# Layer 3 of a four-layer convolution kernel: two lanes of depthwise taps run as whole units, and all other matrix products are gathered between the units

## The chip, the cores and the metric

The kernel runs on one core of a Trainium2 chip. The metric is the device time of one execution in microseconds (us); the times shown are medians of several executions. All data are fp32. TensorE carries out an fp32 matmul in two passes, so in the profile's counts every matmul of the program stands as two MATMUL records, each with a LDWEIGHTS record of its own.

## The reference

The network is four layers on x of shape (4, 48, 256, 256), each with a normalisation before it and a residual after it. Layers 1 and 2 are scans in four directions; layers 0 and 3 are gated feed-forward blocks with a frequency mask. Only layer 3 is touched here:

```python
h = einsum('bchw,oc->bohw', x, w_in)          # 48 -> 288 channels
h = irfft2(rfft2(h in 8x8 patches) * fft_mask) # a mask for each channel
h = depthwise 3x3 convolution of h             # nine taps a channel
x1, x2 = split(h, 2)                           # 144 channels each
y = einsum('bchw,oc->bohw', gelu(x1) * x2, w_out)
```

Since w_in acts on channels and the transform on pixels of a patch, the kernel transforms the 48 input channels first, applies w_in and the mask to the coefficients, and transforms 288 channels back.

## The kernel before: how layer 3 is tiled and what sets the order of its work

`layer3` works through steps of eight image rows, for two images (a and b) at once: 2 pairs of images x (32 full steps + 1 tail step) = 66 steps, 64 of them full. In each full step:

- `normed` (ACT, eight instructions) scales the rows into u; `turned` (TensorE, tiles pt) transposes it into xt; `waves` (tiles pf) transforms it into xf, copied out of PSUM by ACT.
- `spectrum(xf, q)`, once for each of 16 column blocks q, multiplies xf (the weights, 48x128, one for each image) by w_in (288 columns moved) into a tile pz. VectorE then multiplies by the mask into z, in two instructions (128x512 and 128x64).
- `pixels(step, g, k)` transforms z back (tiles pp) into five padded images: z_a0, z_a1 (the first 128 channels of x1 and of x2 of image a), z_b0, z_b1 (of image b), and z_m (what is left over of both). It first copies the two rows above from the step before; then ACT copies each pp tile out, in two instructions of 128x512.
- The depthwise taps. TensorE does those of z_a0, z_a1, z_m and of the lower half of z_b with diagonal 32x32 weights: a `lane` owns two of the four row groups of the array, and one round of a lane is one tap on eight 32x32 tiles. Two lanes fill the sixteen tiles. Nine rounds make a unit, which leaves its sums in a tile pd. The upper half of z_b is done by VectorE: a scaling on ACT, then eight SCALAR_TENSOR_TENSOR a half ("unit", L1220), a gelu and a product.
- `curve` (ACT gelu from pd), `gate` and `lower_gate` (VectorE products from pd, L1203 and L1187) make the gated tiles; `mixed` multiplies them by w_out (tiles po) and adds the residual on VectorE (L1269) before the store.

All of pt, pf, pz, pp, pd and po share one PSUM pool of **four buffers** (`ps_w`), handed out in the order in which they are asked for. Each engine runs its instructions in the order of the program (`manual_schedule`).

That order comes from `in_turns`: after every round of the lanes it adds 0.55 us of credit a lane, and as soon as the credit is not negative it issues the next piece of `work()` (a transpose, a transform, two q of spectra, one `pixels`, a store), each with a hand-written cost. Lane 1 starts four rounds behind lane 0. Pieces therefore fall between tap rounds in many places. `aside` deals out VectorE's taps by the same reckoning. `pixels` of an image has to wait until its last reader is through (`free`, by counts in `taken`).

Of the kernel before, what the change touches and what calls it, by code (L numbers as in the profile page):

```python
# [9 lines left out]
F32 = mybir.dt.float32  # L10
# [7 lines left out]
C = 48  # L18
# [13 lines left out]
class Net:  # L32
# [505 lines left out]
    def in_turns(self, lanes, pieces, pace, side=iter(())):  # L538

        piece, credit, count, ahead, cost = next(pieces), 0.0, 0, 0.0, 1.0
        while lanes or piece:
            moved, spent = 0, 0.0
            for k, l in enumerate(list(lanes)):
                if k == 1 and count < 4:
                    continue
                got = next(l, None)
                if got is None:
                    lanes.remove(l)  # L550
                moved += bool(got)
            count += moved > 0
            spent += 0.54 * moved
            credit = min(credit + pace * moved, 2.0)
            while piece and piece[0]() and (credit >= 0 or not moved):
                piece[2]()
                credit = max(credit - piece[1], -5.0)
                moved, spent = 1, spent + piece[1] - sum(piece[3:])
                piece = next(pieces, None)
            ahead, idle = max(min(ahead + spent, 2.5), -4.0), 0  # L560
            while ahead > 0 or not moved:
                cost = next(side, None)
                if cost:
                    ahead, moved = ahead - cost, 1
                elif cost is None or moved or idle > 20:
                    break
                else:
                    idle += 1
            assert moved or not lanes

    def aside(self, units):

        later, begun = [], set()

        def tick():
            if later:
                later[0][0] -= 1
            while later and later[0][0] <= 0:  # L580
                _, cost, work = later.pop(0)
                work()
                if cost:
                    yield cost

        def begin(k):
            if k < len(units) and k not in begun and units[k][0]():
                begun.add(k)
                units[k][1]()

        for k, (_, _, taps, last) in enumerate(units):
            wait = 0 if k in begun else 2
            while wait:
                begin(k)
                wait -= k in begun
                yield from tick()
                yield 0.0
            for i, (cost, tap) in enumerate(taps):
                if i >= len(taps) - 5:
                    begin(k + 1)  # L600
                tap()
                yield cost
                yield from tick()
            later += [list(e) for e in last]
        while later:
            yield from tick()
            yield 0.0

# [343 lines left out]
    def layer3(self, x, scs):  # L952
# [9 lines left out]
        tail = lambda step: step[1] == H // RB  # L962
        with ExitStack() as st:
# [9 lines left out]
            mk_in = wp.tile([40, 2 * HD], F32, name="mk_in")  # L973
# [4 lines left out]
            mask = wp.tile([128, 1, 2 * HD], F32, name="mask")  # L978
            pm = ps_w.tile([128, 2, MM], F32, name="pm", tag="w")
            nc.tensor.matmul(pm[:, 0, : 2 * HD], self.sel, mk_in, start=True, stop=True)  # L980
            nc.vector.tensor_copy(mask[:, 0], pm[:, 0, : 2 * HD])
# [81 lines left out]
            def turned(u):  # L1063
                xt = mid.tile([128, NQ, 112], F32, name="xt")
                for q0 in range(0, NQ, 8):
                    pt = ps_w.tile([128, 2, MM], F32, name="pt", tag="w")
                    for q in range(8):
                        nc.tensor.transpose(  # L1068
                            pt[:, q // 4, q % 4 * 112 : (q % 4 + 1) * 112],
                            u[:, q0 + q].rearrange("p k e h w -> p (k e h w)"), self.ident[0:112, 0:112],  # L1070
                        )
                    nc.scalar.copy(
                        xt[:, q0 : q0 + 8, :].rearrange("p (k q) c -> p k (q c)", k=2), pt[:, :, 0 : 4 * 112]
                    )
                return xt

            def waves(xt):
                xf = mid.tile([112, NQ, 128], F32, name="xf", tag="u")
                for q0 in range(0, NQ, 8):
                    pf = ps_w.tile([128, 2, 8, 64], F32, name="pf", tag="w")  # L1080
                    for q in range(8):
# [7 lines left out]
                    nc.scalar.copy(  # L1089
                        xf[:, q0 : q0 + 8, :].rearrange("p q (l f) -> p q l f", l=2),  # L1090
# [4 lines left out]
            z = wp.tile([128, NQ, 4 * HD], F32, name="z")  # L1095

            def spectrum(xf, q):

                pz = ps_w.tile([128, 2, MM], F32, name="pz", tag="w")
                for b in range(2):  # L1100
                    s = slice(64 * b, 64 * b + C)
                    nc.tensor.matmul(pz[:, b, 0 : 2 * HD], xf[s, q, :], wi[s, :], start=True, stop=True)  # L1102
                n = 2 * NM
                nc.vector.tensor_tensor(  # L1104
                    z[:, q, 0 : 2 * n].rearrange("p (b c) -> p b c", b=2), pz[:, :, 0:n],
                    mask[:, :, 0:n].to_broadcast([128, 2, n]), ALU.mult,
                )
                nc.vector.tensor_tensor(  # L1108
                    z[:, q, 2 * n :].rearrange("p (h b c) -> p b h c", h=2, b=2),
                    pz[:, :, n : 2 * HD].rearrange("p b (h c) -> p b h c", h=2),  # L1110
                    mask[:, :, n:].rearrange("p o (h c) -> p o h c", h=2).to_broadcast([128, 2, 2, NR]),
                    ALU.mult,
                )
# [3 lines left out]
            def pixels(step, g, k):  # L1117

                n, at, old = (64, 64 * (step[1] % 2), 64 - 64 * (step[1] % 2)) if g == "m" else (128, 0, 0)
# [5 lines left out]
                if tail(step):  # L1125
                    nc.gpsimd.memset(t[:, 2, 1 : W + 1], 0.0)
                    return


                for q0 in range(0, NQ, 8):  # L1130
                    pp = ps_w.tile([128, 2, 8, 64], F32, name="pp", tag="w")
                    for q in range(8):
                        for c in range(n // 64):
                            to, q1 = (slice(64 * (q % 2), 64 * (q % 2) + 64), q // 2) if n == 64 else (
                                slice(64 * c, 64 * c + 64), q
                            )
                            for l in range(2):
                                f = slice(64 * l, 64 * l + 64)
                                nc.tensor.matmul(  # L1139
                                    pp[to, l, q1, :], z[f, q0 + q, k * NM + 64 * c : k * NM + 64 * c + 64],  # L1140
# [3 lines left out]
                        "p h (q j l w) -> p j l q h w", j=128 // n, l=2, w=8  # L1144
                    )
                    for j in range(128 // n):
                        for l in range(2):
                            nc.scalar.copy(  # L1148
                                to[:, j, l], pp[n * j : n * j + n, l, 0 : n // 16].rearrange("p q (h w) -> p q h w", w=8)
                            )  # L1150
# [350 lines left out]
```

## Time and profile before

| | us |
|---|---|
| median of 3 runs (13403.15 to 13455.93) | 13437.11 |
| span of the profiled execution | 13427.3 |
| layers 0 to 2, until about | 8632 |
| layer 3 before its first tap | 59 |
| layer 3, first tap to the end | 4736 |

The profiled execution lies within the spread of the runs. The profile is read by engine (PE is a TensorE matmul, PEld a weight load, DVE VectorE, ACT ScalarE, POOL GpSimd), with busy times as unions of spans. A busy PE is not PE at its peak: a matmul counts from its start to its modelled end, so one short record after another can fill the time. A timeline row has start, length, engine, line, operation, tiles, shape and count, with the idle time before it and what ended that in brackets.

### The profile page before, as it was taken

How to read it: one execution, taken by the hardware profiler on the slowest of the kernel's cores; microseconds unless marked ns; L12 is line 12 of the kernel's file. 1: busy time of each engine (PE TensorE's matmuls, PEld its weight loads, DVE VectorE, ACT ScalarE, POOL GpSimd, SP SyncE). 2: the span in 40 equal slices, each digit the busy share in tenths (PEclk: the TensorE clock that was granted, in tenths of full speed). 3: DMA queues.
4: the chain of work that ended last, by engine and by line, in shares of the span. 5: the costliest groups of instructions: out<-in, count | busy, mean ns of one | idle time of the engine just before them, and what ended most of it. 6: DMA issues, size and time to landing. Idle time of an engine off the chain costs nothing.

```text
span 13427.3 us, 418750 instructions
## 1 busy us (share of the span) xinstructions
PE 12419.8 (92%) x195144; PEld 7348.8 (55%) x195144; DVE 7184.5 (54%) x11691; ACT 3956.8 (29%) x4845; POOL 1336.4 (10%) x977
## 2 busy tenths in 40 slices
PE   2999899998999899999998999799999999999999
PEld 1333333335777677767776777544444454444444
DVE  6777777773333334543333346555555555555555
ACT  1444444442223100012231000044444344444443
POOL 0110010100000003520000025300000000000000
PEclk9999999998999999999999999899999999999999
DMA  7222222225755877977658769501011010011010
GB/s 171 56 56 56 57 54 56 57 49 110 154 138 151 169 151 161 229 165 152 138 154 166 154 147 227 133 19 27 22 27 27 22 28 20 22 27 27 22 27 20
DMA packets 1170327, 1224.12 MB, mean 91 GB/s; under 512 B 1027669, under 2 KB 1031757, under 8 KB 1107725
## 3 DMA queue, kind: packets, MB, share of 16 engines
q1 hardware_dynamic: 1070476, 649.55, 24.8%
q0 software_dynamic: 87488, 445.55, 11.5%
q10 hardware_dynamic: 10624, 102.24, 4.4%
q8 instruction: 1532, 25.10, 0.8%
q14 instruction: 207, 1.69, 0.1%
HBM read 699.76 MB, written 497.42 MB: 89 GB/s over the span
## 4 chain that ended last, share of the span: by engine, by line
PE 47%; ACT 4%; DVE 3%; issue 2%; DMA 0%; SPq 0%; POOL 0%; ACTq 0%; DVEq 0%; POOLq 0%
PE acc L732 20%; PE pd L1160 11%; PE pz L1102 4%; PE pp L1139 4%; PE pd L1176 4%; PE po L1256 2%; ACT u L1056 2%; PE pf L1085 1%; DVE g_b L1187 1%; PE pt L1068 1%; PE po L1246 1%; DVE z L1104 1%; ACT z_a L1148 1%; ACT gl L1186 1%; DVE acc L1220 1%
## 5 line engine op out<-in xcount | busy, mean ns | idle before, releaser
L732 PE MATMUL acc<-line,w_down 96*96 96x256 f32 x12240 | 2692.9, 382 | 52.8 <-ACT line L802 31.5
L732 PEld LDWEIGHTS acc<-line,w_down 96*96 96x96 f32 x12240 | 2008.2, 164 | 729.9 <-DVE line L811 34.2
L1160 PE MATMUL pd<-z_a,diag 32*32 32x512 f32 x37152 | 1862.3, 606 | 45.1 <-issue 31.1
L308 PE MATMUL pd<-main,diag 32*32 32x512 f32 x36864 | 1432.8, 623 | 80.0 <-issue 76.4
L1220 DVE SCALAR_TENSOR_TENSOR acc<-z_b,wd,acc 128x1024 f32<-128x1024 f32 (+1 forms) x1056 | 1328.7, 1260 | 307.0 <-ACT acc L1217 275.0
L732 PE MATMUL acc<-line,w_right 96*96 96x256 f32 x6120 | 1339.4, 379 | 82.0 <-DVE line L882 60.0
L732 PE MATMUL acc<-line,w_left 96*96 96x256 f32 x6120 | 1362.5, 384 | 31.2 <-DVE line L923 31.2
L345 DVE SCALAR_TENSOR_TENSOR acc<-rest,wd,acc 128x1024 f32<-128x1024 f32 x1024 | 1256.7, 1284 | 125.7 <-ACT acc L339 125.4
L732 PEld LDWEIGHTS acc<-line,w_right 96*96 96x96 f32 x6120 | 999.0, 163 | 412.0 <-DVE line L882 61.3
L732 PEld LDWEIGHTS acc<-line,w_left 96*96 96x96 f32 x6120 | 1007.8, 165 | 377.5 <-DVE line L923 47.1
L1176 PE MATMUL pd<-z_b,diag 32*32 32x512 f32 x18432 | 1068.5, 604 | 33.8 <-DVE z L1108 22.0
L1104 DVE TENSOR_TENSOR z<-pz,mask 128x512 f32<-128x512 f32 x1024 | 701.6, 685 | 482.0 <-PE pz L1102 477.4
L811 DVE TENSOR_TENSOR line<-acc,in 96x256 f32<-96x256 f32 x1020 | 429.2, 421 | 961.7 <-PE acc L732 951.6
L308 PEld LDWEIGHTS pd<-main,diag 32*32 32x32 f32 x36864 | 504.7, 105 | 795.6 <-issue 681.0
L885 DVE SCALAR_TENSOR_TENSOR line<-acc,b_right,in 96x256 f32<-96x256 f32 x1020 | 489.4, 480 | 834.9 <-PE acc L732 834.1
L1160 PEld LDWEIGHTS pd<-z_a,diag 32*32 32x32 f32 x37152 | 594.0, 103 | 596.4 <-issue 437.9
L846 DVE SCALAR_TENSOR_TENSOR line<-acc,b_down,in 96x256 f32<-96x256 f32 x992 | 476.0, 480 | 810.8 <-PE acc L732 810.8
L120 ACT ACTIVATE nrm<-nrm 96x2 f32<-96x2 f32 (+2 forms) x5 | 1.0, 203 | 2987.7 <-DVE nrm L119 2987.7
L1139 PEld LDWEIGHTS pp<-c_inv,z 64*64 64x64 f32 x36864 | 603.5, 136 | 465.9 <-issue 262.9
L1139 PE MATMUL pp<-c_inv,z 64*64 64x64 f32 x36864 | 676.1, 222 | 171.7 <-DVE g_b L1187 82.6
L923 DVE SCALAR_TENSOR_TENSOR line<-acc,b_left,in 96x256 f32<-96x256 f32 x992 | 475.8, 480 | 563.8 <-PE acc L732 563.8
L933 POOL TENSOR_TENSOR blk<-blk,line 96x1024 f32<-96x1024 f32 x248 | 705.3, 2872 | 644.0 <-DVE line L923 644.0
(158 smaller groups left out, 12383.8 us busy)
## 6 DMA issues: line engine op xcount, KB each, us to landing
blk<-x ACTq DMA_DIRECT2D x64, 1536.0 KB, 20.2
in<-x SPq DMA_DIRECT2D x248, 384.0 KB, 11.1
dn<-line POOLq DMA_DIRECT2D x124, 768.0 KB, 9.3
rt<-line POOLq DMA_DIRECT2D x124, 768.0 KB, 9.5
in<-rt SPq DMA_DIRECT2D x124, 768.0 KB, 12.6
in<-dn SPq DMA_DIRECT2D x120, 768.0 KB, 5.8
in<-up SPq DMA_DIRECT2D x240, 384.0 KB, 9.9
up<-blk POOLq DMA_DIRECT2D x56, 1536.0 KB, 14.3
```

What stands on the lines that cost most here:

```text
L308: nc.tensor.matmul(pd[32 * j : 32 * j + 32, i], diag[s, t, :], z[s, R2 * j + t // 3 : R2 * j + t // 3 + R2, t % 3 : t % 3 + W], start=(t = ...
L345: nc.vector.scalar_tensor_tensor(to, at(t, r), wd[:, 1, t : t + 1], to, ALU.mult, ALU.add)
L732: self.nc.tensor.matmul(acc, w[:, t, :], carry[:, :, t : t + m], start=(t == 0), stop=(t == 2))
L846: nc.vector.scalar_tensor_tensor(inner(line), acc, bd, new[r], ALU.add, ALU.add)
L885: nc.vector.scalar_tensor_tensor(blocks(inner(line)), blocks(acc), br, new, ALU.add, ALU.add)
L933: (nc.vector if w0 == 0 else nc.gpsimd).tensor_tensor(part, part, inner(ln[:, f::2])[..., lo:hi].rearrange("p w i h -> p i h w"), ALU.add)
L1102: nc.tensor.matmul(pz[:, b, 0 : 2 * HD], xf[s, q, :], wi[s, :], start=True, stop=True)
L1104: nc.vector.tensor_tensor(z[:, q, 0 : 2 * n].rearrange("p (b c) -> p b c", b=2), pz[:, :, 0:n], mask[:, :, 0:n].to_broadcast([128, 2, n]), ...
L1139: nc.tensor.matmul(pp[to, l, q1, :], z[f, q0 + q, k * NM + 64 * c : k * NM + 64 * c + 64], self.inv1[f, :], start=True, stop=True,)
L1160: nc.tensor.matmul(pd[32 * j : 32 * j + 32, i, 0:n, :], diag[s, 2 if g == "m" else half, t, :], zt[g][s, R2 * j + t // 3 : R2 * j + t // 3 ...
L1176: nc.tensor.matmul(pd[to, i], diag[s, half, t, :], zt[f"b{half}"][s, R2 * j + t // 3 : R2 * j + t // 3 + R2, t % 3 : t % 3 + W], start=(t ...
L1220: nc.vector.scalar_tensor_tensor(made[0], at(t), wd[:, half, t : t + 1], made[0], ALU.mult, ALU.add)
```

## The change

- `in_turns` and `aside` are gone from layer 3. The order is written out. `together(k)` runs the nine rounds of one unit of each lane side by side, with five of VectorE's taps dealt out among them; everything else is issued in one group between two such calls. Two steps (an even and an odd one) have seven units a lane, so seven groups.
- z becomes three tiles: zs[0] and zs[1] (the 128 channels of each half, for 16 q and both images) and zr (the rest). `spectrum(xf, k, q0)` makes half k for four q, with w_in's 128 columns moved for each weight; `spectrum_rest` makes the rest for all 16 q, with 32 columns moved. VectorE's mask products have 1024 elements a partition each, nine a step.
- `pixels` takes a string of engines: "A" has ACT copy a pp tile out, "D" VectorE; the same holds for `turned` and `waves`.
- xf no longer shares its buffer with u; a repeated mask (mask_r) is made once at the start.

```diff
-            side = self.aside([unit(s, k) for s in steps for k in range(2)])
-            self.in_turns([lane(0), lane(1)], work(), 0.55, side)
+            def together(k, aside=None):
+                going = [unit(l, *units[l][k]) for l in range(2)]
+                for t in range(9):
+                    for g in list(going):
+                        if next(g, None) is None:
+                            going.remove(g)
+                    if t == 1 and aside is not None:
+                        aside()
+                    if due and (t + 1) * 5 // 9 > t * 5 // 9:
+                        due.pop(0)[1]()
...
+            for n, step in enumerate(steps):
+                even = n % 2 == 0
+                pixels(step, "a0", "AD")
+                if not even:
+                    spectra(n, 1)
+                upper(n, 0, "AD")
+                if even:
+                    turn(n + 1, "AD")
+                together(k, None if even else lambda: ready(n + 1))
+                pixels(step, "a1", "DD")
+                store(n - 1)
+                if fresh(n + 2):
+                    fetch(steps[n + 2])
+                pixels_rest(step)
+                if even:
+                    wave(n + 1, "AA")
+                else:
+                    turn(n + 1, "AA")
+                together(k + 1)
+                upper(n, 1, "AA")
+                if even:
+                    spectra(n + 1, 0)
+                    spectra_rest(n + 1)
+                else:
+                    wave(n + 1, "AA")
+                    spectra(n + 1, 0, slice(0, 2))
+                together(k + 2)
+                k += 3
+                if not even:
+                    spectra(n + 1, 0, slice(2, None))
+                    spectra_rest(n + 1)
+                    spectra(n + 1, 1)
+                    together(k, lambda: ready(n + 2))
+                    k += 1
...
+            zs = [wp.tile([128, NQ, 2, NM], F32, name=f"z{k}", tag=f"z{k}") for k in range(2)]
+            zr = wp.tile([128, NQ, 4 * NR], F32, name="zr")
+            def spectrum(xf, k, q0):
+                pz = ps_w.tile([128, 2, 4, NM], F32, name="pz", tag="w")
+                for q in range(4):
+                    for b in range(2):
+                        s = slice(64 * b, 64 * b + C)
+                        nc.tensor.matmul(
+                            pz[:, b, q, :], xf[s, q0 + q, :], wi[s, NM * k : NM * k + NM], start=True, stop=True
+                        )
+                nc.vector.tensor_tensor(
+                    zs[k][:, q0 : q0 + 4].rearrange("p q b c -> p b q c"), pz,
+                    mask[:, :, :, NM * k : NM * k + NM].to_broadcast([128, 2, 4, NM]), ALU.mult,
+                )
+            def spectrum_rest(xf):
+                pz = ps_w.tile([128, 2, 2 * NQ, NR], F32, name="pz", tag="w")
+                for q in range(NQ):
+                    for b in range(2):
+                        s = slice(64 * b, 64 * b + C)
+                        nc.tensor.matmul(
+                            pz[:, b, 2 * q : 2 * q + 2, :], xf[s, q, :], wi[s, 2 * NM :], start=True, stop=True
+                        )
```

`upper` is `pixels` of z_b0 or z_b1 and the scaling of its upper half; `unit` is nine rounds of one lane with the gelu or gate that follows. An even step gives lane 0 four units (a0, a1, b, m) and lane 1 three, an odd step the reverse, so in the odd steps' units the lanes work on different images.

## The prediction

> **What bounds it now.** The windows view of the stretch from layer 3's first tap (8691) to 13420 comes first: us, then busy time of PE, PEld, DVE, ACT, POOL, then granted clock.
>
> ```profile
> 8691.00:13420.00 4729.00, 4428.70 (x119101) 2256.73 (x119093) 2704.24 (x3974) 1947.55 (x3136) 5.71 (x15) 0.99 0.10 24
> ```
>
> TensorE is busy 94%, VectorE 57%, ACT 41%, and DMA 10%: TensorE sets the pace. 4729 us over 64 full steps are **73.9 us a step**. But busy hides how much of it is work, so I price each kind of run from its start to the start of the next kind, in a stretch of the timeline with no wait:
>
> ```profile
> 10067.10 1.24 PE L1102 MATMUL pz<-wi,xf 48*128 48x288 f32 x8
> 10068.27 1.14 PE L1176 MATMUL pd<-z_b,diag 32*32 32x512 f32 x32
> 10069.34 1.24 PE L1102 MATMUL pz<-wi,xf 48*128 48x288 f32 x8
> ...
> 10072.75 1.14 PE L1176 MATMUL pd<-z_b,diag 32*32 32x512 f32 x32
> 10073.83 2.11 PE L1139 MATMUL pp<-c_inv,z 64*64 64x64 f32 x128
> 10075.87 1.14 PE L1176 MATMUL pd<-z_b,diag 32*32 32x512 f32 x32
> ```
>
> Two q of spectra take 1.17 us (10068.27 - 10067.10), one tap round of both lanes 1.07, a `pixels` 2.04. The chain of waits, in order of time, has the rest (start, us, what):
>
> ```profile
> 10023.85 1.86 PE po L1246 x4
> 10025.71 4.46 PE po L1256 x62
> ...
> 10037.01 1.15 PE pd L1160 x32
> 10038.17 0.82 issue
> 10038.99 1.15 PE pd L1160 x32
> 10040.14 1.68 PE pt L1068 x16
> ```
>
> A store takes 6.3, a transpose 1.7; pf has as many 64x64 records as a `pixels` (8192 / 64 = 128), so 2.0. In a step there are 37152 + 9288 + 18432 = 64872 tap records / 64 / 32 = 31.7 rounds. Unhindered, a step is 31.7 x 1.07 = 33.9 (taps) + 8 x 1.17 = 9.4 (pz) + 4.5 x 2.04 = 9.2 (pp) + 2.0 + 1.7 + 6.3 = **62.5 us. The other 11.4 are waits.** One of them:
>
> ```profile
> 10013.55 1.16 PE L1139 MATMUL pp<-c_inv,z 64*64 64x64 f32 x64
> 10014.38 1.01 ACT L1186 ACTIVATE gl<-pd 64x1024 f32<-64x1024 f32 x1
> 10015.42 0.62 ACT L1124 COPY z_b<-z_b 128x512 f32<-128x512 f32 x1
> 10015.43 1.22 DVE L1187 TENSOR_TENSOR g_b<-gl,pd 64x1024 f32<-64x1024 f32 x1 [8.40 <-ACT gl L1186]
> 10016.07 1.18 ACT L1148 COPY z_b<-pp 128x512 f32<-128x512 f32 x2
> 10016.71 1.02 PEld L1139 LDWEIGHTS pp<-c_inv,z 64*64 64x64 f32 x64 [2.13 <-DVE g_b L1187]
> 10016.71 1.16 PE L1139 MATMUL pp<-c_inv,z 64*64 64x64 f32 x64 [1.99 <-DVE g_b L1187]
> ```
>
> The second pp tile needs the PSUM buffer of a pd; the gate that frees it waits for a gelu, which stood behind eight `normed` instructions on ACT. PE stands still for 2 us in the middle of a `pixels`. The shape recurs: few PSUM buffers, freed by an engine that has something else in its queue.
>
> **Part 1, taps.** Seven units of nine rounds in two steps. Rounds side by side are no cheaper than rounds with pieces between them (1.07 against 4.40 / 4 = 1.10 for four in a row at 10030.17), so no gain is counted: 9 x 1.075 + 0.1 = 9.8 us a unit, **34.3 a step** against 33.9.
>
> **Part 2, spectra.** Before: 64 weight loads a step, 288 columns moved for each. After: 3 x 64 = 192, with 128, 128 and 32. Here the Trainium skill speaks against the change (TensorE: Matmul & The Clock Gate, "LDWEIGHTS (loading the stationary operand)": the load's time goes by the columns of the weights, P / 1.2 ns, whatever the rows). By it each of the 128 added loads is 107 ns; one behind another and exposed, that is +13.7 us a step, and the change would lose. The row next to it is pp: 64 columns loaded and 64 moved, as the new ones have 128 and 128. Its 128 records on four tiles are 32 in succession and take 2.04 us, 0.064 each with the drain. The four 512-column passes at 10023.85 give 1.86 / 4 / 512 = 0.9 ns a column, so 64 moved columns alone are 0.058: the load lies behind the matmul. PEld of pz tells that two loads run at once, one for each image's row group (mean 189 ns each, 351.8 us busy for 4096, so 86 ns each). I take twice pp's pace, 0.115 us a pair: a call for four q has 8 pairs, 0.92 us; the rest has 32 pairs, bound by the load, 3.7 us. A step: 8 x 0.92 + 3.7 + two drains of 0.2 = **11.4** against 9.4. Bounds: 10.5 (0.107 a pair) to 21 (load and matmul in turn).
>
> **Part 3, PE sum.** Groups of two steps, with pp tile pairs at 2.04 (two pairs together 3.9): even 5.6 (a0, b0, pt), 11.4 (a1, store, rest, pf), 9.6 (b1, 4 calls, rest); odd 7.9 (a0, 4 calls, b0), 11.1 (a1, store, rest, pt), 6.1 (b1, pf, 2 calls), 9.4 (6 calls, rest). Sum 61.1, with 7 x 9.8 = 68.6 it is 129.7: **64.9 a step**, 2.4 above the old sum. All gain must come from the 11.4 of waits.
>
> **Part 4, waits that are left.** I walk each group with the four buffers in rotation, gelu 1.05, gate 1.2, two ACT copies of 128x512 1.2 (L1148), a DVE copy taken as L1104's 128x512 product, 0.6 to 0.7, a mask product of 1024 elements taken as L1203's, 1.2, xo 2.7 for eight.
> - Odd group 1: both pd of the b units are held by gelu + gate, one after another (2.7 and 3.9 us after the taps' end); the first pz waits 0.5, the second 0.3; b0's two tiles and both pd then each wait for a mask product (the fourth ends at 10.0). Taps at 10.1 instead of 7.9: **2.2**.
> - Odd group 3: ACT has a gelu, the rows above, four copies of b1 and the scaling of the upper half (1.22) ahead of xf's copy, which ends at 6.8. pz needs it; PE is idle from 4.2. Taps at 9.0 instead of 6.1: **2.9**.
> - Odd group 2: the second pd waits for ACT's four copies of the rest, 12.2 against 11.1: 1.1. Even group 2 likewise 0.7, even 1 0.8 (a gate frees b0's tile), even 3 0.1, odd 4 0.3.
> Sum 8.1 in two steps, **4.0 a step**. VectorE's taps never set the end: five of 1.3 us are 6.5 of a unit's 9.8, and with seven units 35 places stand for 32 taps. VectorE gains 16 x (0.69 + 0.21) - 9 x 1.2 = 3.6 us a step from the wider products and takes eight copies of 0.65; ACT loses those. Both have room (57% and 41%). What these hide costs nothing while a group's queue is shorter than its PE sum; in odd 1 and odd 3 it isn't, and that is counted.
>
> **Part 5, clock.** The windows view after the wait above:
>
> ```profile
> 10013.50:10017.70 4.20, 2.21 (x136) 2.02 (x128) 1.22 (x1) 3.66 (x6) 0.00 (x0) 1.00 0.00 0
> 10017.80:10021.20 3.40, 3.40 (x70) 1.22 (x65) 0.78 (x1) 2.42 (x3) 0.00 (x0) 0.50 0.02 5
> ```
>
> An idle gap of 2 us was followed by 3.4 us at clock 0.50. The same page of the skill ("Why this matters for your kernels") warns of gaps over about 3 us. By the rule the 2.6 us gap of odd group 3 costs nothing; by the row it can cost half of 3.4 us, 1.7 a time, 0.85 a step at the most. The measurement decides that it may happen; I take a little over half, 0.5 a step.
>
> **Sum.** 64.9 + 4.0 + 0.5 = 69.4 against 73.9: 4.5 x 64 = 288 us, so 13427 - 288 = **13,140 us** against the span, which is 10 us under the median of the runs shown. The 59 us before the first tap stay: nine mask products of 1.2 for sixteen pairs of 0.9, against two more pixel tiles and a transpose ahead of the first tap. The DMAs keep their number; `fetch` moves behind the store's four output DMAs on SP, with a landing of 5.1 us and over 40 us until ACT wants it. POOL and SP queue nothing else here.
>
> **Rivals.**
> - A, forecast: 0.70, own range 13,050 to 13,230 (1.4 us a step each way: a pair at 0.107 to 0.125 us, waits of 3 to 5).
> - B, the groups close up: waits almost vanish because the gates leave sooner than I walk. 64.9 a step is 13,427 - 576 = 12,850; halfway 12,980. For it: ACT and DVE have slack. Against it: four buffers. 0.12.
> - C, the waits move and are not removed: gelu, gate and copies of both lanes now fall due at one time, at the end of a unit. 9 us of waits a step (2.6 a group) is no change, 13,430. For it: the g_b wait above has just this shape. 0.10, half of it on a gain of over 0.5% still.
> - D, slower: **the loads are exposed.** Place: the 96 pairs of pz in a step. At 0.23 us a pair instead of 0.115 they cost 11 us more a step, of which odd 1's waits hide about 1: +10 x 64 = 640, 13,780. It decides from 0.162 a pair on (4.5 us over 96 pairs). Against it: pp. 0.05. A clock that halves after nearly every group (3.5 x 1.7 = 6 us a step, 13,490) is 0.03 more.
> - That the order isn't as described is excluded: in the changed kernel's instruction order on TensorE eighteen lots of eight tap matmuls stand in one piece.
>
> A measurement of this kernel tells 0.5% (67 us) from no change. Faster by more: 0.70 + 0.12 + 0.05 = 0.87. Within: 0.05. Slower: 0.08. The range reaches into B's half way and C's: 12,970 to 13,340.
>
> **What would show it.** Taps in runs of 288 records with about 9.8 us to the next kind; pz runs of four calls at 3.7 to 4.0 us and VectorE mask products of 1.2; a wait for an ACT copy of xf ahead of pz in odd steps; PE's sum of waits at 4 a step. Wrong would be: a pz pair over 0.16 us, a unit over 10.5, clock under 0.97 in the layer, or a DVE gate that stands behind its own taps.

## The result, and the profile after

| | us |
|---|---|
| before, median of 4 runs (13403.15 to 13455.93) | 13430.65 |
| after, median of 4 runs (13259.28 to 13288.38) | 13278.57 |
| ratio after / before, 95% interval | 0.9895 (0.9874 to 0.9917) |
| forecast | 13140 (12970 to 13340) |
| span of the profiled execution after | 13257.5, 170 less than before |

The kernel became about 1.1% faster. That lies inside the forecast's range and on its side, but the gain is about half of the 290 us that were forecast: that the range held is luck as far as the mechanism goes, for most of what took the other half was not in the forecast. First the page of after (span, busy time of the engines, clock by slices), then its windows view of layer 3 (us, busy time of PE, PEld, DVE, ACT, POOL, granted clock, DMA share, GB/s):

```profile
span 13257.5 us, 432328 instructions
PE 12356.8 (93%) x203336; PEld 8155.9 (62%) x203336; DVE 7417.3 (56%) x10766; ACT 3602.9 (27%) x4043; POOL 1336.7 (10%) x977
PEclk9999999998999999999999999889999999999999
```

```profile
8691.00:13250.00 4559.00, 4372.60 (x126990) 3054.55 (x126965) 2932.76 (x3064) 1588.13 (x2324) 5.69 (x15) 0.97 0.12 25
```

A full step now takes 4559 / 64 = 71.2 us, where it took 73.9 and 69.4 was forecast. TensorE has some 7,900 matmul records more. One figure moved that the forecast gave little room: the granted clock is 0.97 where it was 0.99.

The waits that the change aimed at did go: by the trace's records of layer 3, TensorE stood idle (stretches of over 0.15 us) for 172 us until a semaphore came before, and for 18 us after. In the groups view of the same stretch (busy us, mean ns of one, then the idle time before and what ended it), `pp` of before lost 82.6 us to the lower gate. After:

```profile
L1139 PE MATMUL pp<-c_inv,z 64*64 64x64 f32 x36761 | 674.5, 222 | 171.7 <-DVE g_b L1187 82.6 <-issue 69.7 <-DVE g_m L1203 15.8
```

```profile
L1043 DVE TENSOR_TENSOR z<-pz,mask 128x1024 f32<-128x1024 f32 x504 | 591.4, 1219 | 272.4 <-PE pz L1040 270.0
L1087 PE MATMUL pp<-c_inv,z 64*64 64x64 f32 x32512 | 557.2, 220 | 50.7 <-issue 49.3
```

The first fence is before, the second after. What is left ahead of `pp` is "issue": the engine waited for nothing that the profile shows. Of such idle time there is more than before, 164 us in the layer instead of 122. The second line above also has the wider mask product at the 1.2 us that the forecast took.

To see where the rest went, every group (all that lies between two tap runs) and every unit (a run of 288 tap records, to the start of the next kind) of the full steps was timed from the trace's records. Means in us:

| after this group | group: forecast | group | unit after it: forecast | unit |
|---|---|---|---|---|
| even 1 (a0, b0, pt) | 6.4 | 7.4 | 9.8 | 9.8 |
| even 2 (a1, store, rest, pf) | 12.1 | 12.1 | 9.8 | **12.4** |
| even 3 (b1, 4 calls, rest of spectra) | 9.7 | 9.9 | 9.8 | **11.3** |
| odd 1 (a0, 4 calls, b0) | 10.1 | 8.5 | 9.8 | 10.2 |
| odd 2 (a1, store, rest, pt) | 12.2 | 11.5 | 9.8 | 10.5 |
| odd 3 (b1, pf, 2 calls) | 9.0 | 8.2 | 9.8 | 9.8 |
| odd 4 (6 calls, rest of spectra) | 9.7 | **11.3** | 9.8 | 9.7 |
| sum | 69.2 | 68.9 | 68.6 | 73.6 |

The groups come out in sum as forecast. The missing gain stands in the units after even 2 and even 3, and inside odd 4. Two of these three have the rest of the spectra in common. The timeline of after, TensorE alone, around an even 3 (start, us, engine, line, operation, tiles, count):

```profile
10284.04 1.97 PE L1087 MATMUL pp<-c_inv,z 64*64 64x64 f32 x117
10286.26 0.44 PE L1087 MATMUL pp<-c_inv,z 64*64 64x64 f32 x11 [0.26 <-issue]
10286.64 3.84 PE L1040 MATMUL pz<-wi,xf 48*128 48x128 f32 x64
10290.31 3.71 PE L1053 MATMUL pz<-wi,xf 48*128 48x32 f32 x64
10293.96 11.24 PE L1139 MATMUL pd<-z_b,diag 32*32 32x512 f32 x288
```

And the windows view of the group, of the next 3.4 us and of the rest of the unit:

```profile
10284.00:10293.90 9.90, 9.64 (x257) 9.39 (x256) 6.20 (x6) 3.60 (x5) 0.00 (x0) 0.99 0.01 3
10294.00:10297.40 3.40, 3.40 (x67) 1.26 (x66) 3.30 (x3) 0.00 (x0) 0.00 (x0) 0.53 0.00 0
10297.50:10305.10 7.60, 7.60 (x239) 5.18 (x222) 4.16 (x4) 0.10 (x1) 0.00 (x0) 1.00 0.02 4
```

The taps' first 3.4 us run at clock 0.53 and 67 records get done in them, where the rest of the unit does 239 in 7.6 us, and this after a group in which TensorE stood still for 0.26 us in all. In odd 4, the same run of the rest is followed by four more calls of spectra, and it is they that are slow, 5.45 us where 64 such records took 3.84 above:

```profile
10075.39 2.06 PE L1040 MATMUL pz<-wi,xf 48*128 48x128 f32 x32
10077.28 3.66 PE L1053 MATMUL pz<-wi,xf 48*128 48x32 f32 x64
10080.77 5.45 PE L1040 MATMUL pz<-wi,xf 48*128 48x128 f32 x64
```

```profile
10075.40:10086.10 10.70, 10.70 (x164) 10.62 (x160) 9.20 (x8) 5.06 (x9) 0.00 (x0) 0.84 0.01 3
```

By the trace's clock records, layer 3 spends 145 us at half clock before and 314 us after. Sorting the stretches by what stands in the 4.5 us ahead of them separates two kinds without exception. Before, all 32 follow TensorE idle time of over 1 us. After, 10 stretches (38 us) do, with over 1.5 us of it, and the other 54 (270 us) follow a run of the rest without any idle time.

The unit after even 2 shows something else:

```profile
10121.18 1.16 PE L1106 MATMUL pp<-c_inv,zr 64*64 64x64 f32 x64
10122.17 2.03 PE L1021 MATMUL pf<-c_fwd_p,xt 64*64 64x64 f32 x128
10124.19 2.12 PE L1123 MATMUL pd<-z_a,diag 32*32 32x512 f32 x39
10128.12 4.45 PE L1123 MATMUL pd<-z_a,diag 32*32 32x512 f32 x128 [1.80 <-issue]
10133.78 1.15 PE L1123 MATMUL pd<-z_a,diag 32*32 32x512 f32 x32 [1.22 <-issue]
```

TensorE stands still twice in the middle of the taps, 1.80 and 1.22 us, and no semaphore ends it. These pauses and the half clock are the two things that the experiments had to explain.

### The profile page after: what moved, and what is told of

Its sections match the earlier page's. It is cut to its first block, busy times and chain, and to the rows that moved or that the text cites. A ratio compares the mean times of both kernels' runs of the same rounds, so it can differ in the third digit from the quotient of the medians.

```text
span 13257.5 us, 432328 instructions
## 1 busy us (share of the span) xinstructions
PE 12356.8 (93%) x203336; PEld 8155.9 (62%) x203336; DVE 7417.3 (56%) x10766; ACT 3602.9 (27%) x4043; POOL 1336.7 (10%) x977
## 3 DMA queue, kind: packets, MB, share of 16 engines
q8 instruction: 1592, 26.08, 0.9%
## 4 chain that ended last, share of the span: by engine, by line
PE 88%; ACT 4%; issue 3%; DVE 3%; DMA 2%; SPq 0%; POOL 0%; DVEq 0%; ACTq 0%; POOLq 0%
PE acc L661 40%; PE pd L1123 12%; PE pd L308 9%; PE pd L1139 5%; PE pz L1040 4%; PE pp L1087 4%; PE po L1215 2%; PE ph L285 2%; PE pz L1053 2%; DMA gx<-in_x 1%; PE ph L277 1%; PE py L382 1%; PE po L452 1%; PE py L389 1%; PE po L1205 1%
## 5 line engine op out<-in xcount | busy, mean ns | idle before, releaser
L1123 PE MATMUL pd<-z_a,diag 32*32 32x512 f32 x37152 | 1626.2, 599 | 57.8 <-issue 49.4
L1123 PEld LDWEIGHTS pd<-z_a,diag 32*32 32x32 f32 x37152 | 890.6, 103 | 604.0 <-issue 232.9
L661 PEld LDWEIGHTS acc<-line,w_right 96*96 96x96 f32 x6120 | 1000.1, 164 | 412.6 <-DVE line L811 61.1
L1139 PE MATMUL pd<-z_b,diag 32*32 32x512 f32 x18432 | 973.7, 642 | 0.5 <-ACT z_b L999 0.5
L1043 DVE TENSOR_TENSOR z<-pz,mask 128x1024 f32<-128x1024 f32 x512 | 601.2, 1219 | 276.2 <-PE pz L1040 273.7
L782 ACT COPY blk<-line 96x1024 f32<-96x1024 f32 (+2 forms) x264 | 480.0, 1891 | 978.0 <-DVE line L775 816.0
L1087 PEld LDWEIGHTS pp<-c_inv,z 64*64 64x64 f32 x32768 | 515.9, 135 | 228.8 <-issue 204.6
## 6 DMA issues: line engine op xcount, KB each, us to landing
in<-rt SPq DMA_DIRECT2D x124, 768.0 KB, 12.6
```

Source lines behind the costliest of these rows:

```text
L661: self.nc.tensor.matmul(acc, w[:, t, :], carry[:, :, t : t + m], start=(t == 0), stop=(t == 2))
L782: nc.scalar.copy(blk[:, :, e, lo:hi, k // 2 : k // 2 + RH], inner(ln[:, e::2])[..., lo:hi].rearrange("p h i w -> p i w h"),)
L1043: nc.vector.tensor_tensor(zs[k][:, q0 : q0 + 4].rearrange("p q b c -> p b q c"), pz, mask[:, :, :, NM * k : NM * k + NM].to_broadcast([128 ...
L1087: nc.tensor.matmul(pp[64 * c : 64 * c + 64, l, q, :], z[f, q0 + q, b, 64 * c : 64 * c + 64], self.inv1[f, :], start=True, stop=True,)
L1123: nc.tensor.matmul(pd[32 * j : 32 * j + 32, i, 0:n, :], diag[s, 2 if g == "m" else half, t, :], zt[g][s, R2 * j + t // 3 : R2 * j + t // 3 ...
L1139: nc.tensor.matmul(pd[to, i], diag[s, half, t, :], zt[f"b{half}"][s, R2 * j + t // 3 : R2 * j + t // 3 + R2, t % 3 : t % 3 + W], start=(t ...
```

## The experiments

Ten kernels ran. For the **half clock** the theories were: IDLE, a gap in which TensorE stands still, as the forecast had it; NARROW, the run of weight loads with only 32 columns moved for each; LENGTH, a long unbroken run of loads, however wide. For the **stalls in the taps**: CODE, TensorE's own instructions arrive too slowly after a burst of short matmuls; DATA, the rows that `fetch` asks for, or the store's output, are in the way of something; BUFFERS, the PSUM waits that the forecast walked.

**Part 2 alone.** `narrow_only` is the kernel before with only the new z tiles and narrow spectra, as eight calls and one piece for the rest in its old order.

```diff
-                    for q in range(0, NQ, 2):
-                        yield always, 1.2, both(*[lambda q=q + i: spectrum(state["xf"], q) for i in range(2)]), 2.0
+                    for k in range(2):
+                        for q0 in range(0, NQ, 4):
+                            yield always, 1.1, lambda k=k, q0=q0: spectrum(state["xf"], k, q0), 1.3
+                    yield always, 3.9, lambda: spectrum_rest(state["xf"]), 1.3
```

> The kernel before, with its own order of work, and only the spectra of the change: z in three tiles, calls for four q with 128 columns moved, and the rest in one piece with 32 columns. By the prediction's second part (loads behind matmuls, 0.115 us a pair) it costs 2.0 us a step: +128 us, ratio 1.010 to the kernel before. By theory CLOCK (the long run of weight loads with 32 columns moved lowers the clock although TensorE is never idle) half-clock time in layer 3 rises from 145 us to over 250 and the ratio is 1.015 to 1.020. By the rival that the shape of the spectra is harmless and that all of the shortfall comes from the new order: ratio 0.997 to 1.003.

Ratio 1.0238 (1.0223 to 1.0254), 13711.02 us: some 315 us slower than before. The spectra themselves cost what was forecast: 1.09 us for a call, 3.69 for the rest, and 683 us of spectra in the layer became 795, +112 where Part 2 says +2.0 x 64 = 128. This is more than was expected by either theory. The other 200 us are not in the products:

```profile
8691.00:13700.00 5009.00, 4652.95 (x126344) 2634.79 (x126320) 2602.99 (x2517) 1918.16 (x3107) 5.57 (x15) 0.95 0.09 23
```

The clock is down to 0.95; half clock went from 145 to 499 us. With the old order the taps lengthened by 68 us in sum and `pixels` by 141. Not all of the half clock is the rest's: 225 us follow a run of the rest with at most 0.3 us of idle time, but 270 us follow idle time of over 1.6 us, for the lower gate now holds `pp` up for longer than the 82.6 us of before:

```profile
PE pp L1155 <- DVE g_b L1200: 191.0, 65, 4.1
```

So the narrow spectra bring half clock of their own, and in the old order they lengthen the waits too. On top of the narrow spectra the rest of the change (the written-out order, the copies on VectorE, xf's own buffer) is worth the distance between the two kernels, 2.4% + 1.05%, some 460 us. What it is worth with the wide spectra was not run.

**IDLE: the rest moved ahead of b1.** In `rest_first`, TensorE's small waits between the rest and the taps change place.

```diff
+                if even:
+                    spectra_rest(n + 1)
                 upper(n, 1, "AA")
                 if even:
                     spectra(n + 1, 0)
-                    spectra_rest(n + 1)
```

> The changed kernel, with spectra_rest of the even steps put at the head of its group, ahead of b1's pixels, so that 2 us of pp and 3.7 us of pz stand between it and the taps. CLOCK: the half-clock stretch moves off the taps; the unit after this group falls from 11.25 us to about 9.8, its group grows by 0 to 1.6; total -50 to 0 us. Rival IDLE (the clock falls because TensorE waits for PSUM buffers or copies in the group): the unit stays at 11.2 us, total within 15 us.

Ratio 0.9878 (0.9863 to 0.9893), not to be told from after. The unit after even 3 falls from 11.3 to 9.7 us, and the group itself rises from 9.9 to 11.0: the slow stretch went with the rest of the spectra, on to what follows it. Half clock 297 us. It is tied to that run and not to the taps. That the gaps are not the cause is read from the records above: 54 stretches with no idle time ahead of them.

**LENGTH and NARROW.** `no_rest` leaves out the products of the rest in every step but the first (the run of loads in a group is then 96 or 64 records, each with 128 columns). `rest64` computes the same as after, with the same 64 records and loads, but moves twice the columns for each, the rest's 32 twice, and reads one copy of the result; for that it takes two PSUM tiles and two mask products of 512 elements where after has one of 1024.

```diff
             def spectra_rest(n):
-                if fresh(n):
+                if fresh(n) and n == 0:
                     spectrum_rest(state["xf"])
```

```diff
             def spectrum_rest(xf):
-                pz = ps_w.tile([128, 2, 2 * NQ, NR], F32, name="pz", tag="w")
-                for q in range(NQ):
+                for q0 in range(0, NQ, 8):
+                    pz = ps_w.tile([128, 2, 8, 2, 2 * NR], F32, name="pz", tag="w")
+                    for q in range(8):
...
+                            nc.tensor.matmul(pz[:, b, q], xf[s, q0 + q, :], wi_2[s], start=True, stop=True)
```

> The changed kernel with spectra_rest in the first step alone; the rest's products of all later steps are left out (zr keeps its first values). It takes 3.7 us of TensorE out of each step. Theory NARROW (the clock falls because the 64 loads with 32 moved columns leave the array empty for two thirds of the time): half-clock time in layer 3 falls from 313 to under 100 us, the even third group's unit from 11.25 to 9.8, the odd last group from 11.3 to about 6; total -290 to -340 us. Theory LENGTH (any run of weight loads over some 5 us does it, also with 128 columns): the odd last group has 96 such records in a row still, half-clock time stays over 150 us, total -220 to -260.

> The changed kernel with the rest's 32 columns moved twice for each weight (64 columns, the second copy unused), in two PSUM tiles with a mask product of 512 elements each. The loads and the time of the run by them stay as they are. NARROW: the array is filled for twice the share of the time, half-clock time falls to under 200 us, total -30 to -80. LENGTH: half-clock time stays over 280 us, total within 20.

`no_rest`: 0.9655 (0.9637 to 0.9674), half clock 38 us. LENGTH falls with it: runs of up to 96 loads with 128 columns don't bring it. `rest64`: 0.9823 (0.9802 to 0.9843), 13154.34 us, half clock 114 us instead of 314. Its timeline at the same place in an even step, then in an odd 4, and the windows view of the 3.4 us after the even group:

```profile
10385.38 2.20 PE L1093 MATMUL pp<-c_inv,z 64*64 64x64 f32 x128
10387.52 3.84 PE L1040 MATMUL pz<-wi,xf 48*128 48x128 f32 x64
10391.19 3.69 PE L1059 MATMUL pz<-wi,xf 48*128 48x64 f32 x64
10394.81 9.76 PE L1145 MATMUL pd<-z_b,diag 32*32 32x512 f32 x288
...
10324.04 2.06 PE L1040 MATMUL pz<-wi,xf 48*128 48x128 f32 x32
10325.93 3.69 PE L1059 MATMUL pz<-wi,xf 48*128 48x64 f32 x64
10329.45 3.79 PE L1040 MATMUL pz<-wi,xf 48*128 48x128 f32 x64
```

```profile
10394.80:10398.20 3.40, 3.40 (x113) 1.93 (x122) 3.21 (x4) 0.00 (x0) 0.00 (x0) 1.00 0.00 0
```

The rest takes 3.69 us with 64 columns as it took 3.71 with 32: it is the load that sets its pace. But the unit after it is 9.76 us instead of 11.24, the four calls 3.79 instead of 5.45, and 113 records get done where 67 did. Over the layer a half-clock stretch touches what follows the rest in 12 of 62 cases, where it was 54 of 62. TensorE does more work and the kernel is 0.7% faster. That is the strongest single result here: the half clock after the rest comes from how little is moved for each load.

**The spectra in halves of 144.** `halves144` drops the rest as a product of its own: each half of w_in is moved whole, 144 columns for each weight, in calls of three, three and two q, and VectorE makes two products of each call. There are 128 weight loads a step instead of 192.

```diff
-            parts = [(0, 0, NM), (HD, NM, NM), (NM, 2 * NM, NR), (HD + NM, 2 * NM + NR, NR)]
+            parts = [(0, 0, 2 * HD)]
...
-                            pz[:, b, q, :], xf[s, q0 + q, :], wi[s, NM * k : NM * k + NM], start=True, stop=True
+                            pz[:, b, q * HD : q * HD + HD], xf[s, q0 + q, :], wi[s, HD * k : HD * k + HD],
+                            start=True, stop=True,
```

> The changed kernel with the rest made together with its half: 144 columns moved for each weight, calls of 3, 3 and 2 q, no run with 32 columns, 128 loads a step instead of 192; one half of the odd steps' k = 1 calls moves from the last group to the next step's first; VectorE has two products a call. CLOCK: half-clock time in layer 3 falls from 313 to under 150 us and the unit after the even third group from 11.25 to 9.8. With 64 pairs of 0.13 us a step instead of 96 of 0.115 the total falls by 100 to 250 us, less where VectorE's products (about 10 us in the odd step's last group) become late. Rival (the clock follows idle gaps, not the narrow columns): half-clock time stays over 250 us, total -50 to -150.

Ratio 0.9772 (0.9757 to 0.9787), 13087.81 us, half clock 37 us: **faster than both kernels**. Its layer 3 by the windows view:

```profile
8691.00:13055.00 4364.00, 4136.21 (x122061) 2790.32 (x122054) 2964.32 (x3998) 1579.85 (x2313) 5.68 (x15) 1.00 0.13 26
```

VectorE has some 900 instructions more than in after and is busy 32 us longer; TensorE is busy 236 us less.

**DATA: what is in flight during the stalls.** `fetch_later` writes `fetch` after the unit that follows group 2, instead of in the group. `wave_later` moves the even step's `wave`, with the 128 short records of pf, to the same place.

```diff
                 store(n - 1)
-                if fresh(n + 2):
-                    fetch(steps[n + 2])
                 pixels_rest(step)
...
                 together(k + 1)
+                if fresh(n + 2):
+                    fetch(steps[n + 2])
```

```diff
-                if even:
-                    wave(n + 1, "AA")
-                else:
+                if not even:
                     turn(n + 1, "AA")
                 together(k + 1)
+                if even:
+                    wave(n + 1, "AA")
                 upper(n, 1, "AA")
```

> The changed kernel, with the loads of the raw rows (fetch) issued one group later, behind the unit of a1. Theory DATA (TensorE's code packets are late because the raw rows' packets are under way at the same time): the unit after the even step's second group falls from 12.4 to about 10.4 us, the odd one's from 10.45 to about 9.9; total -60 to -100 us. Theory CODE (TensorE runs out of code because the group spends 776 instructions in 12 us and packets of 256 come no closer than 3.3 us; the raw rows don't matter): unit stays at 12.0 to 12.6, total within 20 us.

> The changed kernel, with the even step's pf (128 records, 256 instructions) moved from the second group to the head of the third. CODE: the second group's unit falls from 12.4 to about 10.4 us and its group from 12.1 to about 9.9; the third group grows from 9.9 to 12 to 13.5 (pf and a wait for xf's copy); total -80 to 0 us. DATA alone: the unit stays at 12 or more, total 0 to +60 us.

`fetch_later`: 0.9887 (0.9868 to 0.9907); the unit after even 2 stays at 12.6 us. But this says nothing against DATA, for the rows did not move. SP still issues them around the store's output: each of the layer's 120 row DMAs within 2.0 us of one of the store's, in after within 1.7. One place in the timeline of `fetch_later`, SP alone:

```profile
10270.52 0.32 SPq L981 DMA_DIRECT2D raw<-x  x1
10271.47 3.59 SPq L1235 DMA_DIRECT2D out<-xo  x4
10275.12 0.42 SPq L981 DMA_DIRECT2D raw<-x  x1
```

`wave_later`: 0.9889 (0.9872 to 0.9905); the unit falls from 12.4 to 10.8 and the group ahead of it by 2.6, but even 3 rises from 9.9 to 14.1, by 4.2, where pf itself is 2.0. The stalls went where the short records went, and their sum over the layer (pauses of over 0.9 us that no semaphore ends) stayed at 127 us. That speaks for CODE.

**CODE.** The page of every kernel has a DMA queue of instructions; that of after (packets, MB, share of the engines' time):

```profile
q8 instruction: 1592, 26.08, 0.9%
```

26.08 MB in 1592 packets are 16 KB each. The trace's packets of layer 3 number 995, for 253,955 records of PE and PEld: one packet for every 256. They follow one another at 4.03 us in the median and never under 3.24. A unit uses 576 records in 9.8 us, one packet in 4.4 us, just inside what arrives. The 192 matmuls with their 192 loads before it are 1.5 packets in 3.0 us. In after TensorE stands idle for over 0.9 us 88 times with no semaphore at the end, 127 us in sum, and 5 times, 7 us, until a semaphore comes. Before it was 42 times (55 us) and 80 times (119 us).

A count of the records settles what the 88 are. Each begins when the number of TensorE's records done (loads, matmuls and its own waits) is 256 times the number of code packets landed by the pause's end, plus 193: the same remainder 88 times, so at the boundary of a packet. Each ends 1.19 to 1.82 us after that packet landed. The same holds for the 42 of before, and for none of the 5 and 80 that a semaphore ends. The engine had used up its code and went on when the next packet was there.

Why the packet isn't there is not the same in all places. In the 46 long pauses of even 1 and odd 3 no rows are in flight. The awaited packet landed 2.2 us (median) after TensorE had begun the 256 records before it, and TensorE goes on some 1.4 us later, but short matmuls use 256 records up in 2.1 to 2.7 us: here the burst alone is too fast. In the 27 of the unit after even 2 (40.5 us) TensorE takes 4.0 us (median) over the 256 records, the packet landed only after 4.0, and meanwhile the rows of the store and of `fetch` keep the DMA engines 99% busy. The DMA view of 10122 to 10130 shows it (packets, MB, share):

```profile
q1 hardware_dynamic: 3168, 1.53, 98.7%
q8 instruction: 1, 0.02, 1.2%
```

By an estimate from these figures, a packet that landed after 2.2 us would have let TensorE go on at 3.6, in time. So DATA is a part of the answer in even 2: the rows delay the code. `wave_later` shows that they need the burst as well (6 long pauses, 7 us, in that unit without pf). No run moved the rows, so their part is read from the trace and not tested.

`half_code` tests it: `pixels` issues one matmul of 128 columns where it had two of 64, so half the instructions for the same columns. It leaves out the transform of every second column block (the first of each pair is written twice).

```diff
-                    for q in range(8):
+                    for q in range(0, 8, 2):
...
-                                    pp[64 * c : 64 * c + 64, l, q, :], z[f, q0 + q, b, 64 * c : 64 * c + 64],
-                                    self.inv1[f, :], start=True, stop=True,
+                                    pp[64 * c : 64 * c + 64, l, q : q + 2, :], z[f, q0 + q, b, 64 * c : 64 * c + 64],
+                                    inv2[f], start=True, stop=True,
```

> The changed kernel, but in pixels of a0, a1, b0 and b1 each weight is met by 128 moved columns (the inverse transform twice) instead of 64, and only every second column block is transformed; the transform of the other blocks is left out. TensorE's array time stays[...], as do all copies and PSUM tiles; the instructions of a pixels fall from 256 to 128. CODE: the first groups fall (even 7.4 to 5.5 or so, odd 8.5 to 7.5 or so), the stalls of over 0.9 us that end just after a code packet fall from 107 to under 60, total -100 to -200 us. Rival BUFFERS (the groups' excess over the sum of TensorE's work is waits for PSUM buffers, gates and copies, as the prediction had it): groups stay, total within 40 us.

Ratio 0.9854 (0.9839 to 0.9868). Even 1 in the timeline of after, and then of `half_code`:

```profile
10242.18 3.48 PE L1087 MATMUL pp<-c_inv,z 64*64 64x64 f32 x205
10247.03 1.03 PE L1087 MATMUL pp<-c_inv,z 64*64 64x64 f32 x51 [1.36 <-issue]
10247.99 1.75 PE L1006 MATMUL pt<-c_ident,u 112*128 112x112 f32 x16
```

```profile
10080.61 4.08 PE L1090 MATMUL pp<-inv,z 64*64 64x128 f32 x128
10084.62 1.75 PE L1009 MATMUL pt<-c_ident,u 112*128 112x112 f32 x16
...
10045.31 3.64 PE L1043 MATMUL pz<-wi,xf 48*128 48x128 f32 x32 [1.15 <-ACT xf L1002]
```

The pause of 1.36 us is gone and the group takes 5.69 us every time, the bare PE sum of Part 3 (5.6), where it took 7.4. CODE is shown for this group. Even 2, where the burst has the rest and pf in it and not `pixels` alone, keeps its unit of 12.4. Over the layer long pauses without a semaphore fall from 127 to 61 us, and those with one rise from 7 to 50: the last line, in an odd 3, is the wait for ACT's copy of xf that the forecast had walked. Behind the code stalls the BUFFERS waits stood ready. Part of the gain is given back by the clock, at half speed for 386 us here, so the whole kernel gains less than was expected.

**pf inside a unit.** `wave_inside` issues pf's matmuls after the fifth round of taps, so that no burst stands alone; `wave_inside_144` does the same to `halves144`.

```diff
+                    if t == 4 and inside is not None:
+                        inside()
...
-                together(k + 1)
+                together(k + 1, None, wave(n + 1, "AA"))
```

> The changed kernel, but pf (256 instructions in 2 us) stands in the middle of the a1 unit, after its fifth round, in even and odd steps, instead of in a group. CODE: its instructions fall where TensorE spends 256 in 4.3 us; group and unit of the even step's second fall together from 24.6 to 22 us or so, the odd third group from 8.2 to 5 to 6 while the unit before it grows by 2; total -40 to -130 us. BUFFERS or none: the work only changes its place, total within 20 us.

> Both of the last two. If their mechanisms are apart, the gains add up: -140 to -350 us against the changed kernel. If both only move the same wait, no more than the larger of the two.

0.9872 (0.9855 to 0.9888) and 0.9768 (0.9754 to 0.9783), 13077.8 us. Neither can be told from the kernel it starts from. The long pauses for code do become fewer in `wave_inside`, 57 with 77 us instead of 88 with 127, but group and unit of even 2 make 24.2 us together with pf inside, against 24.6. The gains that were expected of spreading the burst did not come.

## Why the prediction missed: point by point

The step came to 71.2 us instead of 69.4. Place by place, over two steps, this is +5.0 in the units and -0.3 in the groups, less the 1.0 that the forecast had set aside for the clock: 3.7, or 1.8 a step.

- **The step that failed first is Part 5, the clock**, 0.5 us a step after an idle gap in odd 3. That gap mostly isn't there: odd 3 takes 8.2 us instead of 9.0, and in the whole layer TensorE waits for xf 9.6 us instead of 2.6 us in every odd 3. What halves the clock is the rest of the spectra, twice in two steps: 1.5 us in the unit after even 3 and 1.6 in odd 4, together 1.5 a step. `rest64`, which changes little else, wins 0.7%, some 96 us or 1.5 a step: the same figure by another way. 1.0 of the 1.8 is this term, with the wrong trigger and a third of its size. I had weighed the Trainium skill's rule on idle gaps (TensorE: Matmul & The Clock Gate, "Why this matters for your kernels") against a row with a gap, and both speak of TensorE standing still. Here it does not stand still.
- **Part 1, 9.8 us a unit**, is right for an undisturbed unit (median 9.68 after even 1, odd 3 and odd 4) and wrong as a mean (10.5). I had taken it that a unit is a piece of its own, whose time doesn't depend on the group ahead. After even 2 it is 2.6 longer, for the most part because code comes late in it (1.5 us a time is idle time that no semaphore ends). The 0.4 and 0.7 after odd 1 and odd 2 are of another kind: one lane begins alone, because the first load of the other waits for a PSUM buffer, 0.6 us a time for a mask product and 0.45 for ACT's copies of the rest. `half_code`, with less code in these groups, does not shorten them (10.5 and 10.7).
- **Part 4, the waits**, is near in sum and wrong in kind. 8.1 us in two steps were walked, as gates, gelus and copies that hold PSUM buffers. Measured are 6.2 in the groups (68.9 - 61.1 - 1.6 of clock) and 3.7 in those three units, 9.9 in all: 0.9 a step more. About half of it is TensorE standing still with no semaphore at the end (164 us in the layer, 5.3 in two steps), a term that the forecast put at nothing. The code stalls stand in the places of the walked waits and cover them, and a walked wait comes back when the code is halved. What was walked right is that a unit's start after odd 1 and odd 2 hangs on a mask product and on the copies of the rest; only one lane waits, not both. With the clock's 1.0 this makes the 1.8 up, within rounding.
- **Part 2 and rival D.** 0.115 us a pair holds (64 records in 3.67 to 3.84 us, the rest in 3.65 to 3.7), and the loads lie behind the matmuls. The price of the spectra by themselves was right within 16 us of 128. What they cost beyond that, the clock, was not in Part 2 at all.
- **Part 3** needs no change: even 1 in `half_code` shows its bare sum. But the 11.4 us a step that the forecast called waits, from which all gain was to come, were not all TensorE standing still: by its first line that is 4729 - 4429 = 300 us, 4.7 a step. The rest was work above its price; the taps took 39.4 a step, not 33.9. (A slip without weight: half way to rival B is 12,995, not 12,980.)
- **Rivals B and C.** The semaphore waits went as B says (119 us of long pauses to 7), and something else came in their place as C says, but not gelu and gate: in the waits view the gate on L1150 waits for its gelu 221 us in layer 3, where it was 620.

```profile
DVE g_b L1187 <- ACT gl L1186: 620.5, 113, 9.9
```

```profile
DVE g_b L1150 <- ACT gl L1149: 220.9, 94, 5.5
PEld pd L1123 <- issue: 242.7, 547, 3.2
PEld pp L1087 <- issue: 203.3, 251, 2.1
PEld pd L1123 <- ACT z_m L1113: 20.0, 45, 0.7
PEld pd L1123 <- DVE z L1043: 17.9, 23, 0.9
PE pz L1040 <- ACT xf L999: 9.6, 15, 1.4
```

The first fence is before, the second after (total us, times, longest). After, the long rows of the weight loads end with "issue"; the last three rows are what is left of the walked waits.

Of the signs that the forecast named as wrong, two turned up, at the places of these causes: a mean unit over 10.5 after even 2 and after even 3, and a clock at its bound of 0.97.

## What to carry to other kernels

Price a matmul with a full weight load and few moved columns not only by its own time but by the clock of what follows it, and look in a window of some 3.4 us behind it: here widening a product (`rest64`) or merging it into a wider one (`halves144`) costs TensorE nothing or less and wins 0.7% to 1.2%. Count the instructions of a stretch beside its microseconds: where short matmuls use up 256 records in 2.1 us, or where rows in flight hold the next packet back, TensorE stalls, sometimes only in the next piece of work, with "issue" as its only trace. That the pauses all fall at the same place of a 256-record packet tells them from other waits. And when waits on buffers are removed from an engine that is busy over 90%, ask which limit of that engine itself stands right behind them.

## What the runs showed of the hardware

- **Half clock without idle time.** 64 records with 128 columns of weights and 32 moved columns each (3.7 us in which TensorE's rows have no gap) are followed by 3.4 or 6.8 us at half clock, in 84% of the even steps. With 64 moved columns, or with runs of 128 or 144 alone, it mostly stays away: 314 us of half clock in the layer become 114 in `rest64`, 38 in `no_rest` and 37 in `halves144`. An estimate from the rows: at 0.9 ns a column (the 512-column pass shown in the forecast) the array moves data in 0.029 of each 0.115 us with 32 columns (a pair of records, one in each row group), 25%, and 50% with 64. The Trainium skill (TensorE: Matmul & The Clock Gate, "Part 1: The HAM clock gate") has the clock follow how busy TensorE has been, in windows of about 3.4 us, and the length of the slow stretches agrees. That "busy" means moving columns and not loading weights is what these runs suggest; where the bound lies between 25% and 50% they don't tell.
- **Instructions as a resource.** Code comes in 16 KB packets of 256 records, 4.03 us apart in the median and at least 3.24. All 88 long pauses that no semaphore ends stand at the boundary of a packet and end 1.19 to 1.82 us after the next one landed. From the first record of one packet to the landing of the next it took 2.2 us where no rows were in flight and 4.0 us in the unit after even 2, with the DMA engines 99% busy (medians of the packets waited for). What sets the distance of the packets was not tried.
